# Last mixture of experts: wider token rows, routing straight from the logits, another order of loads, a shared expert in two parts, and sums on three engines

## The chip, the core and the metric

The kernel runs on one core of a Trainium2 chip. The engines are called by short names: PE (TensorE, matrix products), PEld (its weight loads), DVE (VectorE), ACT (ScalarE), POOL (GpSimd), SP (SyncE, which here only issues transfers). The metric is the device time of one execution in microseconds (us); smaller is better. Times given inside an execution are microseconds from the start of its profiled span.

## The reference

Four layers of attention and feed-forward work over x[1024, 256], each followed by a residual sum and a layer norm. The change concerns the last feed-forward, a mixture of 64 experts:

```
logits = h @ router_w.T                       # h: [1024, 256] -> [1024, 64]
probs  = softmax(logits)
top_vals, top_idx = top_k(probs, 8)
top_vals = top_vals / sum(top_vals)
comb   = zeros(1024, 64) with top_vals at top_idx
for each expert e:                            # 2 x 64 hidden columns
    g, u = split(h @ gate_up[e].T)
    out += (silu(g) * u) @ down[e].T * comb[:, e]
shared = sigmoid(h @ shared_gate_w.T) * (silu(h @ Sg.T) * (h @ Su.T)) @ Sd.T
x = layernorm(x + out + shared)
```

## The kernel before, in words

The stages run one after another (`STAGES`). Inside a block under `in_order(transfers=True)` every engine, SP's queue included, executes in the order in which the program is written, so a place in the text is a place in each queue.

**Clearing.** `clear_rows` (L1366 to L1376), called at the start of the feed-forward of the third layer, makes a table in device memory of 64 experts x 1024 rows of `ROW` numbers (L46, here 256 + 3 x 8 = 280, so 1,120 bytes) and fills it with zeros by 64 transfers on POOL's queue.

**Routing, `close` (L1983 to L2085).** It is a generator: every `yield` ends a step, and `close_on` (L2089) makes one step wherever the attention code or its drain calls it, so the routing of a tile of 128 tokens is spread over the last attention's work. Tiles 0 to 3 go two at a time (n = 2), 4 to 7 singly; a generator is made by `add_up` (L2244) once a tile's attention output is summed, and the generators run one after another. The steps for a tile: root of the variance (`power`, L231: a DVE operation and a power on POOL), norm, three steps apart the transposes (L2009), the copy of the transpose (L2013), the router's logits (L181), a full softmax (L2022 to L2029), the eight largest by `max` and `match_replace` (L2033 to L2035, which gives the 0/1 mask `taken`), gates normalised over the eight (L2037 to L2040, `comb`), then two products on PE that count for every token how many earlier tokens chose each expert (L2043, L2047), and the row places (L2054 to L2071). Last, for each tile, a one-hot comparison of 8 x 64 gathers the eight gates in the order of the places (L2076, L2080, L2084). A row thus holds 256 numbers of the token, 8 expert numbers, 8 result addresses, 8 gates. Each tile then goes out by eight indirect scatters on POOL (L151, `table<-w`), one row per token and chosen expert; `close_on` sends one a call, or two once the attention is drained.

**Experts, `ffn3` (L2408).** SP first loads five of eight pieces of the weights (`weights_for`, L2425: two transfers of gate/up and one of down, 512 KB each, for four pairs of experts). `shared_expert` (L2300) is computed whole and added to `k.x`, then `more_blocks` (L2332) works out which experts have more than 128 rows (98 and up) and need extra blocks. `run` (L2598) goes through 16 groups of four experts ("own") and six extra groups ("more") among them. A group's rows are loaded two groups ahead (`load`, L2443; groups 1, 3 and 5 first issue another piece of weights). Each group has two units; a unit is turned on PE (`turn`, L2522, copy on DVE L2524), multiplied with gate and up (`hidden`, L2533, with silu on ACT L2540 and a product on DVE L2541), turned again if it is an extra one (`turn_hidden`), multiplied with the down weights (`down`, L2576), scaled by its gate on ACT (L2582) and scattered by POOL to its result rows (L151, `results<-y,sel`): 64 such scatters for own units, 12 for extra ones. `find` (L2490) picks for each row its address and its gate by comparing the row's eight expert numbers with the expert at hand. After `run`, an `If` (L2629), which is not taken with these inputs, would do further extra blocks; its branch costs each engine some time.

**Last sums, `add_results` (L2633).** Eight loads of 1 MB each bring a tile's eight results per token (the last in four parts); tiles 2, 4 and 6 are summed by three halving additions on DVE (L2643) and one more (L2644), the others by nine products with the identity on PE (L2648). DVE takes the statistics (L2669, L2670), `power` the root, DVE the final product (L2656), and ACT's queue issues the output's write (L2657).

Of the kernel before, what the change touches and what calls it, by code (L numbers as in the profile page):

```python
# [33 lines left out]
P = 128  # L34
# [11 lines left out]
ROW = D + 3 * K3  # L46
# [1894 lines left out]
def attn3(k, a):  # L1941
# [41 lines left out]
    def close(t, n):  # L1983
# [3 lines left out]
        rstd = k.power(stats[t // 4][:, at : at + n, 1], n, LN_EPS, tag="root")  # L1987
        yield
# [5 lines left out]
        rows, probs, comb, order = part(0, ROW), part(560, 64), part(688, 64), part(912, 8)  # L1994
        taken = work[:, 816 : 816 + 32 * (n + 1)].bitcast(BF16)
        taken = taken.rearrange("p (i e) -> p i e", e=E3)
        place = part(928, 8).bitcast(I32)
# [4 lines left out]
        nc.vector.memset(taken[:, n, :], 0.0)  # L2002
        yield
        yield
        yield
# [7 lines left out]
        nc.vector.tensor_copy(k.xT[:, :, PAD + t * P : PAD + (t + n) * P], ps)  # L2013
        yield
# [7 lines left out]
        nc.vector.tensor_reduce(low, logits, axis=AX.X, op=ALU.max, negate=True)  # L2022
        nc.vector.tensor_tensor(probs, logits, low.unsqueeze(2).to_broadcast(shape), ALU.add)
        nc.scalar.activation(probs, probs, AF.Exp)
        nc.scalar.activation(gate, ps[:, :, 64], AF.Exp, scale=-1.0)
        yield
        nc.vector.tensor_reduce(total, probs, axis=AX.X, op=ALU.add)
        nc.vector.reciprocal(inv, total)
        nc.vector.tensor_tensor(probs, probs, inv.unsqueeze(2).to_broadcast(shape), ALU.mult)  # L2029
        yield  # L2030
        for i in range(n):
            top = k.tile("st", [P, 8])
            nc.vector.max(top, probs[:, i, :])  # L2033
            nc.vector.match_replace(comb[:, i, :], top, probs[:, i, :], -1.0)
        nc.vector.tensor_scalar(taken[:, :n, :], comb, 0.0, None, ALU.is_lt)  # L2035
        yield
        nc.vector.tensor_tensor(probs, probs, taken[:, :n, :], ALU.mult)  # L2037
        nc.vector.tensor_reduce(total, probs, axis=AX.X, op=ALU.add)
        nc.vector.reciprocal(inv, total)
        nc.vector.tensor_tensor(comb, probs, inv.unsqueeze(2).to_broadcast(shape), ALU.mult)  # L2040
        yield
# [10 lines left out]
        yield  # L2052

# [4 lines left out]
        nc.vector.tensor_tensor(base, ps[:, n, :], base, ALU.add)  # L2058
        for i in range(n):
            nc.vector.max(order[:, i, :], probs[:, i, :])  # L2060
        yield
# [4 lines left out]
        for i in range(n):  # L2066
            nc.vector.tensor_scalar(
                rows[:, i, D + K3 : D + 2 * K3], dest, float((t + i) * P * K3), None, ALU.add
            )
# [3 lines left out]
        shape = [P, K3, E3]  # L2073
        for i in range(n):
            eq = k.tile("t2", [P, K3, E3])
            nc.vector.tensor_tensor(  # L2076
                eq, probs[:, i, :].unsqueeze(1).to_broadcast(shape),
                order[:, i, :].unsqueeze(2).to_broadcast(shape), ALU.is_equal,
            )
            nc.vector.tensor_tensor(  # L2080
                eq, eq, comb[:, i, :].unsqueeze(1).to_broadcast(shape), ALU.mult
            )
            yield
            nc.vector.tensor_reduce(rows[:, i, D + 2 * K3 :], eq, axis=AX.X, op=ALU.add)  # L2084
            sending.extend((place[:, i, m : m + 1], rows[:, i, :]) for m in range(K3))  # L2085
# [158 lines left out]
    def add_up(g, b, oT):  # L2244
        project_heads(k, b, oT, ws[g][1])
        if g == 3:
            if b % 4 == 0:
                stats[b // 4] = k.tile("st", [P, 4, 2], tag="stats", bufs=2)
            k.add_stats(b, stats[b // 4])
            if b > 3:  # L2250
                k.closing.append(close(b, 1))
            elif b % 2:
                k.closing.append(close(b - 1, 2))
        yield 4 * D * COLUMN
# [6 lines left out]
    with k.in_order(transfers=True):  # L2261
# [30 lines left out]
        for _ in pipe.drain():  # L2292
            close_on()
        k.drained = True
# [5 lines left out]
def shared_expert(k, gate_up, down):  # L2300


    nc = k.nc
    g, u = k.bank(), k.bank()
    for j, ps in enumerate((g, u)):
        for c in range(NC):
            for half in range(2):
                nc.tensor.matmul(
                    ps[64 * half : 64 * half + 64, :],
                    lhsT=gate_up[:, c, 64 * j : 64 * j + 64],  # L2310
                    rhs=k.xcols(c, half * HALF, HALF), start=c == 0, stop=c == NC - 1,
                )
    h = k.tile("shared", [P, HALF])
    nc.scalar.activation(h, g, AF.Silu)
    nc.vector.tensor_tensor(h, h, u, ALU.mult)
    for t in range(4):
        ys = k.wide()
        for half in range(2):
            rows = slice(64 * half, 64 * half + 64)
            nc.tensor.matmul(  # L2320
                ys[:, half * HALF : half * HALF + D], lhsT=h[rows, t * P : (t + 1) * P],
                rhs=down[rows, :], start=True, stop=True,
            )
        for half in range(2):
            at = 4 * half + t
            nc.vector.scalar_tensor_tensor(
                k.x[:, at, :], ys[:, half * HALF : half * HALF + D], k.gate[:, at : at + 1],
                k.x[:, at, :], ALU.mult, ALU.add,
            )


def more_blocks(k, ids, column):  # L2332
# [26 lines left out]
    columns = small([P, 2])  # L2359
# [6 lines left out]
    expert, start, held, row = (small([P, 2]) for _ in range(4))  # L2366
# [41 lines left out]
def ffn3(k, a):  # L2408
# [27 lines left out]
    for lo in range(0, 20, 4):  # L2436
# [6 lines left out]
    def load(group):  # L2443
        kind, g = group
        xr = rows[group] = k.tile("xr", [P, 4, ROW])
        if kind == "own":
            if g in (1, 3, 5):
                weights_for(20 + 2 * (g - 1))
            nc.sync.dma_start(
                out=xr, in_=regions[4 * g : 4 * g + 4, :P, :].rearrange("e p w -> p e w")  # L2450
            )
# [38 lines left out]
    def find(group):  # L2490
# [3 lines left out]
        at = slice(n * g, n * g + n)  # L2494
        mine = ids[:, at] if kind == "own" else keys[:, at]
        waste = (spare if kind == "own" else spare[:, E3:])[:, at]
        eq, both = k.tile("sel", [P, n, K3]), k.tile("sel", [P, n, 2, K3])
        pair, off, index = (k.tile("sel", m) for m in ([P, n, 2], [P, n], [P, n]))
# [5 lines left out]
        nc.vector.tensor_tensor(  # L2504
            both, xr[:, :, D + K3 :].rearrange("p h (w k) -> p h w k", k=K3),
            eq.unsqueeze(2).to_broadcast([P, n, 2, K3]), ALU.mult,
        )
        nc.vector.tensor_reduce(pair, both, axis=AX.X, op=ALU.add)
        nc.vector.scalar_tensor_tensor(
            off, pair[:, :, 0], 0.0, waste, ALU.is_equal, ALU.mult  # L2510
        )
        nc.vector.scalar_tensor_tensor(index, pair[:, :, 0], -1.0, off, ALU.add, ALU.add)
        found[group] = index, pair
# [54 lines left out]
    def down(unit):  # L2568
        (kind, g), i = unit
        hT, ys, yt = hs.pop(unit), k.wide(), k.tile("y", [P, 2, D])  # L2570
        index, pair = found[kind, g]
        halves = [slice(64 * h, 64 * h + 64) for h in range(2)]
        ys = ys.rearrange("p (r n) -> p r n", r=2)
        if kind == "own":
# [5 lines left out]
            for h in range(2):  # L2580
                at = 2 * i + h
                nc.scalar.activation(  # L2582
                    yt[:, h, :], ys[:, h, :D], AF.Copy, scale=pair[:, at, 1:2]
# [9 lines left out]
        nc.scalar.activation(yt[:, 0, :], ys[:, 0, :D], AF.Copy, scale=pair[:, i, 1:2])  # L2593
# [4 lines left out]
    def run(groups):  # L2598
# [5 lines left out]
        turn(units[0])  # L2604
        for at in range(len(units) + 2):
# [6 lines left out]
            if at < len(units):  # L2612
# [3 lines left out]
            if 0 < at <= len(units):  # L2616
# [170 lines left out]
```

## Time and profile before

| what | us |
|---|---|
| median of the three runs shown (2069.09 to 2073.79) | 2070.15 |
| the profiled execution, whole | 2065.07 |
| its span, first to last instruction | 2063.4 |
| PE busy / DVE busy / ACT busy / POOL busy in the span | 1830.1 / 1314.5 / 884.0 / 695.4 |
| mean granted PE clock | 0.950 |

The page's groups give for every line its engine, operation, output and input by the program's names, how often, busy time, mean time of one in ns, and the idle time of that engine just before. Those of the part that is changed:

```profile
L151 POOL DMA_INDIRECT results<-y,sel x76 | 73.9, 973 | 44.0 <-ACT y L2582 25.5
L151 POOL DMA_INDIRECT table<-w x64 | 64.8, 1012 | 49.1 <-DVE root L235 19.4
L1374 POOL DMA_DIRECT2D table<-zero x64 | 34.1, 534 | 132.3 <-DMA table<-zero 132.3
```

A timeline row has the start, the duration, engine, line, operation, output and input, the count merged into the row, and in brackets how long the engine was idle before and what ended that. A row of the windows has the stretch, its length, the busy time and count of PE, PEld, DVE, ACT and POOL, the granted clock, the share of the DMA engines in use, and the rate in GB/s.

### The profile page before, as it was taken

The numbers are of one execution on the slowest core, as the hardware profiler recorded it, in microseconds if no ns is written. First come the engines' busy times: TensorE is split into PE (matmuls) and PEld (weight loads), VectorE is DVE, ScalarE is ACT, GpSimd is POOL, SyncE is SP. The second block draws the span as 40 slices with busy tenths as digits, with TensorE's granted clock in tenths as the row PEclk, the third lists the DMA queues.
The fourth block names the chain that finished last, engine by engine and source line by source line (L and its number), as shares of the span: only waits on it lengthen the run. The fifth ranks groups of instructions, "written<-read, shape, count | busy, mean of one in ns | idle before, by whom it ended". The sixth has DMA issues, their size and how long they took to land. (4 is left out here: it accounts for less than half of the span.)

```text
span 2063.4 us, 26548 instructions
## 1 busy us (share of the span) xinstructions
PE 1830.1 (89%) x8329; PEld 1143.1 (55%) x8329; DVE 1314.5 (64%) x2873; ACT 884.0 (43%) x2410; POOL 695.4 (34%) x934
## 2 busy tenths in 40 slices
PE   8988759699999989989889989999999998885995
PEld 4655535456666666576444344444666655554654
DVE  5788846667876766545467444453667665865573
ACT  3666614445343343445344622227535454331460
POOL 5343222333333332233021131104333325554472
PEclk9999969899999999998999999999999999997897
DMA  6322254344454553401050089970344423446855
GB/s 184 81 69 75 66 164 133 95 110 124 111 146 107 157 148 93 99 10 62 21 175 2 2 348 419 426 307 25 88 115 110 100 54 98 109 106 240 288 181 216
DMA packets 173651, 281.88 MB, mean 137 GB/s; under 512 B 36000, under 2 KB 133664, under 8 KB 164416
## 3 DMA queue, kind: packets, MB, share of 16 engines
q1 hardware_dynamic: 146832, 161.45, 28.4%
q0 software_dynamic: 25520, 117.60, 15.2%
q8 instruction: 70, 1.15, 0.2%
q10 hardware_dynamic: 1152, 1.05, 0.1%
q14 instruction: 77, 0.63, 0.1%
HBM read 87.75 MB, written 109.71 MB: 96 GB/s over the span
## 5 line engine op out<-in xcount | busy, mean ns | idle before, releaser
L174 PE MATMUL bank<-xT,w 128*128 128x512 f32 (+1 forms) x960 | 390.2, 546 | 3.0 <-DVE xT L200 2.8
L389 DVE STREAM_TRANSPOSE turned<-p 128x128 f32<-128x128 f32 (+7 forms) x232 | 283.7, 1223 | 107.0 <-POOL p L285 59.7
L285 POOL TENSOR_SCALAR p<-p,st 128x128 f32<-128x128 f32 (+7 forms) x256 | 190.4, 744 | 462.1 <-DVE st L284 460.6
L292 PE MATMUL wide<-k,q 128*128 128x512 f32 (+3 forms) x768 | 300.9, 502 | 15.4 <-ACT p L277 14.4
L426 PE MATMUL bank<-pt,v 128*128 128x256 f32 x1216 | 287.4, 379 | 13.5 <-DMA pt<-turned 11.1
L426 PEld LDWEIGHTS bank<-pt,v 128*128 128x128 f32 x1216 | 230.9, 195 | 68.6 <-issue 26.8
L174 PEld LDWEIGHTS bank<-xT,w 128*128 128x128 f32 x960 | 183.7, 196 | 147.4 <-issue 129.7
L269 DVE TENSOR_REDUCE st<-wide 128x1 f32<-128x128 f32 (+7 forms) x256 | 193.4, 756 | 42.2 <-PE wide L297 35.5
L292 PEld LDWEIGHTS wide<-k,q 128*128 128x128 f32 x768 | 141.6, 194 | 134.5 <-issue 95.0
L277 ACT ACTIVATE p<-wide,st 128x128 f32<-128x128 f32 (+7 forms) x128 | 94.8, 741 | 239.0 <-DVE st L269 213.4
L277 ACT ACTIVATE p<-wide,st,factor 128x256 f32<-128x256 f32 (+7 forms) x128 | 106.3, 831 | 101.6 <-POOL st L274 96.3
L264 DVE TENSOR_TENSOR wide<-wide,causal 128x128 f32<-128x128 f32 x192 | 56.0, 292 | 104.2 <-PE wide L292 103.3
L807 ACT ACTIVATE e<-wide,st 128x128 f32<-128x128 f32 x256 | 89.8, 377 | 74.6 <-DVE st L815 65.2
L181 PE MATMUL bank<-w,xT 128*128 128x512 f32 (+2 forms) x288 | 116.2, 539 | 3.4 <-DVE xT L2013 2.0
L1682 ACT ACTIVATE pt<-wide 128x1024 f32<-128x1024 f32 (+3 forms) x96 | 75.6, 810 | 69.8 <-PE wide L1676 67.9
L151 POOL DMA_INDIRECT results<-y,sel x76 | 73.9, 973 | 44.0 <-ACT y L2582 25.5
L1685 POOL TENSOR_SCALAR_AFFINE_SELECT pt<-pt 128x256 f32<-128x256 f32 x64 | 25.9, 406 | 183.2 <-ACT pt L1682 182.8
L151 POOL DMA_INDIRECT table<-w x64 | 64.8, 1012 | 49.1 <-DVE root L235 19.4
L1374 POOL DMA_DIRECT2D table<-zero x64 | 34.1, 534 | 132.3 <-DMA table<-zero 132.3
L181 PEld LDWEIGHTS bank<-w,xT 128*128 128x128 f32 x288 | 52.1, 195 | 47.2 <-issue 37.5
L1634 DVE TENSOR_REDUCE st<-wide 128x2 f32<-128x1024 f32 x64 | 64.3, 1020 | 18.1 <-PE wide L1623 8.9
L873 PE MATMUL bank<-w,ot 128*128 128x256 f32 x256 | 64.6, 398 | 7.8 <-ACT ot L867 5.3
(401 smaller groups left out, 3237.5 us busy)
## 6 DMA issues: line engine op xcount, KB each, us to landing
table<-zero POOLq DMA_DIRECT2D x64, 1120.0 KB, 21.9
pt<-turned SPq DMA_DIRECT2D x60, 240.0 KB
pt<-turned SPq DMA_DIRECT2D x60, 176.0 KB
pt<-turned SPq DMA_DIRECT2D x156, 64.0 KB
xr<-table SPq DMA_DIRECT2D x16, 560.0 KB
gu<-in_L_ffn_gate_up_dram SPq DMA_DIRECT2D x16, 512.0 KB
pt<-turned SPq DMA_DIRECT2D x28, 256.0 KB
r<-results SPq DMA_DIRECT2D x7, 1024.0 KB
```

Of the source, the lines that this page charges most:

```text
L151: self.nc.gpsimd.indirect_dma_start(out=views.pop(), out_offset=bass.IndirectOffsetOnAxis(ap=index, axis=0), in_=source, in_offset=None,)
L174: self.nc.tensor.matmul(out, lhsT=weight(c), rhs=self.xcols(c, lo, n), start=c == 0, stop=c == NC - 1)
L181: self.nc.tensor.matmul(out, lhsT=self.xcols(c, lo, n), rhs=weight(c), start=c == 0, stop=c == NC - 1)
L269: nc.vector.tensor_reduce(top, scores[:, :n], axis=AX.X, op=ALU.max, negate=True)
L277: nc.scalar.activation(probs[:, :n], scores[:, :n], AF.Exp, bias=top, scale=1.0 if scale is None else scale, accum_out=total,)
L285: self.nc.gpsimd.tensor_scalar(probs[:, :n], probs[:, :n], total, 1.0, ALU.mult, ALU.mult)
L292: self.nc.tensor.matmul(s[:, lo : lo + m], lhsT=query, rhs=key(lo, m), start=True, stop=not masked or lo + m < n, skip_group_check=masked,)
L389: k.nc.vector.transpose(squares.rearrange("p b (k q) -> p b k q", q=32), probs[:, :n].rearrange("p (k i b) -> p b k i", b=4, i=32),)
L426: self.k.nc.tensor.matmul(out.rearrange("p (a q) -> p a q", q=32) if first else out.rearrange("p (s a q) -> p s a q", s=2, q=32), lhsT=val ...
L807: nc.scalar.activation(e[:, r, f, b, :], sc[:, r, f, b, :], AF.Exp, bias=top[:, at : at + 1], accum_out=total[:, at : at + 1],)
L873: nc.tensor.matmul(y, lhsT=oT[:, i % 2 * 2 + i // 2].rearrange("p b n -> p (b n)"), rhs=wo[:, i, :], start=i == 0, stop=i == 3,)
L1682: nc.scalar.activation(two[:, :, lo:], sc[:, :, lo:], AF.Exp)
```

## The change

Rows carry all 64 gates instead of eight picked ones, so `ROW` is 256 + 16 + 64 = 336 numbers (1,344 bytes), the one-hot gathering goes, and `comb` is written straight into the row. The eight largest are found among the logits; the exponent is taken with the largest subtracted, and only the masked exponents are summed. The steps of `close` are fewer and in another order, the last tile's root is issued at once in `add_up`, and the drain makes two steps per call. In `ffn3` six pieces of weights precede the rows, the first group's rows come in two transfers, and groups 1 and 3 issue their piece of weights after their rows. `find` reads the gate from the row's column, or for extra groups selects it among 64. Own units go to `down` one round sooner. The shared expert's gate half is computed before `run` and the rest after it. The last sums go to PE (tiles 1, 4, 7), POOL (2, 5) and DVE (0, 3, 6); the root is ACT's square root, and ACT makes the final product.

```diff
-ROW = D + 3 * K3
+ROW = D + 2 * K3 + E3
...
-    def close(t, n):
+    def close(t, n, rstd=None):
-        rstd = k.power(stats[t // 4][:, at : at + n, 1], n, LN_EPS, tag="root")
-        yield
+        if rstd is None:
+            rstd = k.power(stats[t // 4][:, at : at + n, 1], n, LN_EPS, tag="root")
+            yield
...
+        comb = rows[:, :, D + 2 * K3 :]
...
-        yield
-        yield
+        if n > 1:
+            yield
+            yield
...
+        nc.vector.memset(taken[:, n, :], 0.0)
+        for i in range(n):
+            nc.vector.tensor_scalar(
+                rows[:, i, D + K3 : D + 2 * K3], dest, float((t + i) * P * K3), None, ALU.add
+            )
...
-        nc.vector.tensor_reduce(low, logits, axis=AX.X, op=ALU.max, negate=True)
-        nc.vector.tensor_tensor(probs, logits, low.unsqueeze(2).to_broadcast(shape), ALU.add)
-        nc.scalar.activation(probs, probs, AF.Exp)
...
+        for i in range(n):
+            nc.vector.max(order[:, i, :], logits[:, i, :])
+            nc.vector.match_replace(probs[:, i, :], order[:, i, :], logits[:, i, :], NEG)
+        nc.vector.tensor_tensor(taken[:, :n, :], probs, logits, ALU.not_equal)
+        nc.vector.tensor_scalar(low, order[:, :, 0], -1.0, None, ALU.mult)
         yield
         for i in range(n):
+            nc.scalar.activation(probs[:, i, :], logits[:, i, :], AF.Exp, bias=low[:, i : i + 1])
+        nc.scalar.activation(gate, ps[:, :, 64], AF.Exp, scale=-1.0)
...
-        for i in range(n):
-            eq = k.tile("t2", [P, K3, E3])
...
-            yield
-            nc.vector.tensor_reduce(rows[:, i, D + 2 * K3 :], eq, axis=AX.X, op=ALU.add)
...
+            if b == NT - 1:
+                rstd = k.power(stats[b // 4][:, b % 4 :, 1], 1, LN_EPS, tag="root")
+                k.closing.append(close(b, 1, rstd))
...
         for _ in pipe.drain():
             close_on()
+            close_on()
...
-    for lo in range(0, 20, 4):
+    for lo in range(0, 24, 4):
         weights_for(lo)
...
         if kind == "own":
-            if g in (1, 3, 5):
-                weights_for(20 + 2 * (g - 1))
-            nc.sync.dma_start(
-                out=xr, in_=regions[4 * g : 4 * g + 4, :P, :].rearrange("e p w -> p e w")
-            )
+            step = 4 if g else 2
+            for lo in range(0, 4, step):
+                at = 4 * g + lo
+                nc.sync.dma_start(
+                    out=xr[:, lo : lo + step, :],
+                    in_=regions[at : at + step, :P, :].rearrange("e p w -> p e w"),
+                )
+            if g in (1, 3):
+                weights_for(22 + 2 * g)
             return
...
+        combs = xr[:, :, D + 2 * K3 :]
+        if kind == "own":
+            scales = [combs[:, i, n * g + i : n * g + i + 1] for i in range(n)]
+        else:
...
+            nc.vector.tensor_tensor(
+                picked, ids.unsqueeze(1).to_broadcast(shape),
+                mine.unsqueeze(2).to_broadcast(shape), ALU.is_equal,
+            )
+            nc.vector.tensor_tensor(picked, picked, combs, ALU.mult)
+            nc.vector.tensor_reduce(scale, picked, axis=AX.X, op=ALU.add)
...
         turn(units[0])
+        hidden(units[0])
+        find(units[0][0])
...
-            if 0 < at <= len(units):
-                turn_hidden(units[at - 1])
-            if at > 1:
-                down(units[at - 2])
+            for unit in units[at - 1 : at] if at else ():
+                if unit[0][0] == "own":
+                    down(unit)
+                else:
+                    turn_hidden(unit)
+            for unit in units[at - 2 : at - 1] if at > 1 else ():
+                if unit[0][0] != "own":
+                    down(unit)
...
-        shared_expert(k, shared, shared_down)
+        shared = Shared(k, shared, shared_down)
         where, keys, sides, longest = more_blocks(k, ids, column)
+        shared.gate()
...
         run([group for _, group in sorted(own + more)])
+        shared.up()
+        shared.add()
...
+    def sums(t, e):
         r, y = rs[t], k.x[:, t, :]
...
+    def measure(t):
+        six, two = k.tile("st", [P, 6]), k.tile("st", [P, 2])
+        nc.vector.bn_stats(six, ys[t])
+        nc.vector.bn_aggr(two, six)
+        root = k.tile("st", [P, 1])
+        nc.scalar.activation(root, two[:, 1:], AF.Sqrt, bias=k.eps[LN_EPS])
+        stats[t], roots[t] = two, root
+
+    def finish(t):
+        root, shift, z = roots[t], k.tile("st", [P, 1]), k.tile("z", [P, D])
+        nc.vector.reciprocal(root, root)
+        nc.vector.scalar_tensor_tensor(shift, stats[t][:, :1], -1.0, root, ALU.mult, ALU.mult)
+        nc.scalar.activation(z, ys[t], AF.Identity, bias=shift, scale=root)
+        nc.sync.dma_start(out=k.out[t * P : (t + 1) * P, :], in_=z)
...
+        for lo, n in ((0, 4), (4, 2), (6, 2)):
+            load(NT - 1, lo, n)
+        for t in (1, 4, 7):
+            sums_on_pe(t)
+        for t in (2, 5):
+            sums(t, nc.gpsimd)
+        sums(0, nc.vector)
+        measure(0)
+        measure(1)
+        finish(0)
+        sums(3, nc.vector)
+        finish(1)
+        measure(2)
+        measure(3)
+        finish(2)
+        finish(3)
+        measure(4)
+        sums(6, nc.vector)
+        finish(4)
+        measure(6)
+        measure(5)
+        finish(6)
+        measure(7)
+        finish(5)
+        finish(7)
```

`Shared.gate` projects the shared expert's gate half and applies silu, `Shared.up` projects the other half and multiplies, `Shared.add` multiplies with the down weights and adds to `k.x`; they hold the operations of `shared_expert`.

## The prediction

> **What bounds the kernel now.** I read the slices first (the change touches only the last 170 us of 2063.4, and the clearing of the table near 1200 to 1380), then the chain of waits there, POOL's timeline, and the windows. The chain shows what starts the experts:
> ```profile
> 1906.36 2.44 DMA table<-w
> 1908.86 0.38 SPq L2449
> 1910.91 8.23 DMA xr<-table
> ```
> The last row scatter starts at 1906.36, lands 2.44 us later, only then is the first row read issued; the second read waits 8.23 us behind 1.5 MB of weights. How the last tile comes so late, and what follows it, is in the timeline:
> ```profile
> 1883.38 0.14 DVE L235 TENSOR_SCALAR root<-stats 128x1 f32<-128x1 f32 x1
> 1896.06 0.69 DVE L2084 TENSOR_REDUCE w<-t 128x8 f32<-128x512 f32 x1
> 1897.51 0.96 POOL L151 DMA_INDIRECT table<-w  x1 [3.31 <-issue]
> ...
> 1926.49 0.95 POOL L151 DMA_INDIRECT results<-y,sel  x1 [19.17 <-ACT y L2582]
> ...
> 2024.31 0.96 POOL L151 DMA_INDIRECT results<-y,sel  x1 [0.30 <-issue]
> ...
> 2027.92 17.33 SPq L2665 DMA_DIRECT2D r<-results  x11
> ...
> 2059.95 0.54 DVE L2656 TENSOR_SCALAR z<-bank,st,st 128x256 f32<-128x256 f32 x1 [0.44 <-POOL st L236]
> ```
> Tile 7's root waits for tile 6's gate gathering; its own ends at 1896.75. The results' scatters run from 1926.49 to 2025.27: 98.8 us for 76, where 76 x 1.266 (pitch: 0.96 busy, 0.30 idle) is 96.2. So POOL sets the experts' end, and its first scatter sets POOL. After that the reads take 2.46 us a tile, and DVE works until 2060.49, 11 us after the last read.
>
> **The end of attention: costed at 0.** The gate gathering goes (0.67 + 0.69 + 0.64 = 2.0 us of DVE a tile), and so does the full softmax (five operations, some 1.0 us). Rows are sent six steps sooner. Why this may pay:
> ```profile
> 1849.66 1.99 DVE L389 STREAM_TRANSPOSE turned<-p 128x1024 f32<-128x1024 f32 x1 [3.87 <-POOL p L285]
> ...
> 1853.99 0.69 PE L2009 MATMUL bank<-ident,x 128*128 128x128 f32 x2 [3.64 <-DVE st L284]
> ```
> Three scatters (1844.89 to 1848.47) stood on POOL before the product that DVE waited for, and PE stood 3.64 us. Against it: single tiles lose two empty steps before their transposes, so PE, in written order, reaches them sooner and waits on the norm sooner. A stall removed is worth 3.64, plus the slow clock after it (scores 3.62 against 1.88, sixteen value products 5.06 against 3.67), in all 6.8. Bounds: 6.8 gained, or 6.8 lost on each of tiles 4, 5 and 6. I take 0, as both ends rest on the same stall.
>
> **Tile 7's rows.** Its root follows its statistics (1881.26): +0.21 to the DVE operation, +0.25 to POOL's power, +0.60 to the norm, all as for tile 6 from 1852.46: 1882.32, before 1886.69. From norm to first use of the logits 2.96 as before: 1885.28. Then maximum, replacement and mask 0.82 (1891.16 to 1891.98), the negated maximum 0.19, exponent on ACT 0.4, four operations to the gates 1.07, the ranks 1.1: 1888.9. Then 0.76 to the first scatter, as from 1896.75 to 1897.51: 1889.6, which is 7.9 sooner. Tile 6's eight scatters (10.1 us) fit into POOL's idle 19.45 us before 1883.74. Tile 7's eighth starts at 1898.5; those from 1883 to 1900 took 5.5 to 6.2 us to land beside weights, so 1904.3.
>
> **The reads still wait, for the weights ahead of them.** Six pieces stand ahead instead of five: 6 x 1.573 MB, 0.26 for the shared expert, 8 x 0.172 for tile 7's scatters (rows of 1,344 bytes for 1,120): 11.08 MB.
> ```profile
> 1880.00:1890.00 10.00, 2.08 (x8) 1.22 (x6) 4.30 (x12) 0.41 (x1) 5.13 (x6) 0.69 1.00 359
> 1890.00:1900.00 10.00, 5.81 (x18) 1.82 (x18) 6.35 (x25) 2.19 (x4) 5.21 (x6) 0.63 1.04 403
> ```
> The last two columns are DMA share and GB/s: full. They carry 7.62 MB by 1900; the other 3.46 at 403 GB/s end at 1908.6. Half a group (0.344 MB) takes 0.85, and 0.15 to PE: the first turn at 1909.6, before 1913.18. The other rows follow at once, so the 2.24 us that PE stood before 1919.27 go too. Bounds: 1905.5, if rows overtake weights, and 1913, if nothing is won. What moves on SP's queue: the sixth piece's three issues (1.6 us as at 1909.29 to 1910.86) fall into its idle 1893.5 to 1908.8, one more read issue costs 0.4 behind the full DMA queue, nothing on the path; the last pieces' issues now stand behind reads.
>
> **To the first result.** PE at its slow clock: turn 0.97, wait for the copy 0.85, products 1.98, two turns 1.94, products 1.9, then 1.43 from the start of the down product (1925.06) to the scatter (1926.49): 9.1. First scatter 1918.7, 7.8 sooner; the same 98.8 us bring the last to 2017.5. PE as a check: it took 105.45 us (1913.18 to 2018.63), less 2.24: 2012.8, plus about 3 for the last copies and scatters, 2015.8. POOL stays ahead of it as the bound, by little. Bounds for POOL's gaps: none (2014.9), or PE no longer ahead and 7 us of gaps (2021.9, the wait for a first result being 7.8 less than it was).
>
> **Costed at nothing.** Clearing: 20% more bytes. The fills' pitch is 2.93 us (161.1 over 55), so 55 x 0.59 = 32.2 us more.
> ```profile
> 1359.69 0.53 POOL L1374 DMA_DIRECT2D table<-zero  x1 [2.29 <-DMA table<-zero]
> 1396.09 1.03 POOL L236 TENSOR_TENSOR st<-st,minus_half 128x4 f32<-128x4 f32 x1 [35.87 <-DVE st L235]
> ```
> The queue behind them is free until 1396.09; the last fill would be issued by 1392.4 and land by 1418, before the next transfer on SP's queue (1427.29). The cover is 3.7 us; every further us is lost. Extra groups pick their gate from 64: three operations of 0.29 (L2362, L2367) six times, 5.2 us of DVE, which is busy 7.13 of 8 us at its fullest there; POOL's backlog covers it. Last weights behind the rows: units 24 and up come late. Up projection and sum after the run: 2.7 (half of 5.47) + 0.8 + 3.34 = 6.8 us from 2012.8 to 2019.6, and DVE's branch 3.1 (2017.6 to 2020.7): 2022.7, against a first result tile at 2024.9. If that cover goes, up to 4 us of DVE's wait for PE's first sum covers the rest. ACT's table loads once more (1.28, as at 1897.53), in that same wait. The eight output writes go from ACT's queue to SP's, idle after the reads.
>
> **The last sums.** Reads start 2.65 us after the last scatter ends: R = 2020.2. Tiles land at R + 4.7, then each 2.46 (R + 21.9 for the last). DVE adds three tiles at 2.86 each and measures eight (0.65); power on POOL is replaced by a root on ACT and two small DVE operations (0.35); the 0.47 of the product moves to ACT. New waits: ACT's product waits for DVE's shift, and a later tile's root queues behind it on ACT, for which DVE's next reciprocal waits: 0.5 at most each, and only in the last two tiles without other DVE work between. PE's tile 1, cold, ends at R + 13.2 as tile 0 took 6.1, so DVE's third starts at 14.3. POOL's adds: 1.27 for 512 elements (L1895), so 5.1 a tile, R + 9.6 to 14.7 and 17.0 to 22.1. Freely, DVE's order then ends in z at R + 27.3. But two engines add at once, and this trace shows what that does:
> ```profile
> 122.31 3.27 DVE L823 SCALAR_TENSOR_TENSOR diff<-e,st 128x128 f32<-128x128 f32 x4
> 122.32 2.60 POOL L627 TENSOR_TENSOR k<-t,t 64x512 f32<-64x512 f32 x2
> ...
> 132.05 1.14 DVE L823 SCALAR_TENSOR_TENSOR diff<-e,st 128x128 f32<-128x128 f32 x4
> ```
> The four DVE operations take 1.14 alone and 3.27 beside POOL. At R + 17.1 the small products of tile 1's and later shifts stand behind POOL's 2.54, 1.27 and twice 0.64, and tile 6's add slips with them: about 2.4, z at R + 29.7. With 2.9 from the last z to the end (as 2060.49 to 2063.4): R + 32.6, where before took 35.5. I take the locked value; the bounds are 30.2, and 36 if every DVE addition waits.
>
> The Trainium skill (SBUF — State Buffer, "Who interferes with whom") says that a DVE instruction with two SBUF inputs contends with a GpSimd one that reads SBUF, and that whoever issues first keeps the port for a whole instruction. It speaks against giving POOL a share of the sums: by it each such DVE addition can lose up to one POOL instruction. The row above agrees; by the rule the sum is the locked one, without it 2.4 us less.
>
> **Sum.** 2020.2 + 32.6 = 2052.8 against the span of 2063.4: 10.6 us less, of which 7.8 lie before R and 2.9 after it. That execution took 2065.07, the runs shown have a median of 2070.15. Rounding the saving to 11: 2059.
>
> **Rivals.** More: the stall at 1850 goes, with its clock, 6.8, and the lock costs nothing, 2.4: 2050. For it: POOL's three scatters would be sent before. Against: the shorter way to the transposes. Hidden: PE, not POOL, ends the experts, since it no longer runs 13 us ahead of the first scatter; 7 of 7.8 us come back as gaps on POOL and only the tail's 2.9 stay: 2070.15 - 3.7 = 2066.5. For it: from 1990 PE is busy 8.00, 7.87 and 8.00 of 8 us. Against: POOL is at its pitch for the first 48 scatters. Slower: the transposes, two steps sooner, stop PE on the norms of tiles 4, 5 and 6 in turn, 6.8 us each with the clock: 2059 + 20.4 = 2079. It decides from 3.7 us a tile on; PE already stood 2.14, 2.67 and 3.64 there. Against: it was the late scatters that made the longest of them. Does not do what it says: the fills outgrow their cover, 40% slower instead of 20%: 55 x 1.17 = 64 us later less 35.9 of cover, 28: 2087.
>
> **How the numbers follow.** Forecast 0.60 (its own range 2052 to 2065), more 0.18, hidden 0.10, slower by stalls 0.09, by fills 0.03. Within 0.2% (4.1 us, about what a measurement of this kernel can tell) is 2066.0 to 2074.3: that is the hidden case. Faster 0.78, same 0.10, slower 0.12. The range 2048 to 2068 takes in the forecast, the hidden case and most of "more".
>
> **What would show it.** First results scatter near 1918.7 after the same attention, first turn near 1909.6, 76 scatters in 97 to 101 us, reads-to-end 32 to 33 us, POOL's power near 1396 unmoved. Wrong it is if PE's waits on the transposes grow past 3.7 us a tile, if the fills end after 1396, or if POOL shows more than 7 us of gaps between results.

## The result, and the profile after

Timed beside each other on one chip, the changed kernel takes 2077.32 us (median of 15, 2070.99 to 2086.41) and the kernel before 2067.13 us (median of 15, 2060.18 to 2074.73): ratio 1.005, 95% interval 1.0033 to 1.0068. The change costs some 10 us where 11 us less were forecast. The profiled execution of the changed kernel took 2070.99 us, the least of its 15; its span is 2069.3 us.

Three places split both spans into four stretches: POOL's first power of attn3 (1396.09 before, 1391.84 after), the first transposed transfer on SP's queue (1427.29 and 1441.52), the addition of tile 7's attention output (line L255, 1880.34 and 1894.04), and the first read of results (2027.92 and 2035.96).

| stretch | before | after | difference |
|---|---|---|---|
| power to first transposed transfer | 31.20 | 49.68 | +18.5 |
| from there to tile 7's addition | 453.05 | 452.52 | -0.5 |
| tile 7's addition to first result read | 147.58 | 141.92 | -5.7 |
| first result read to the end | 35.5 | 33.3 | -2.1 |

The sum, +10.2, is as large as the difference of the medians (up to the power this execution happened to be 4.3 us ahead, so the spans differ by 5.9). So the last two stretches, at which the change aims, did gain 7.8 us in these two executions. The loss stands 450 us ahead of them, at the start of the last attention. This is the timeline of the changed kernel there:

```profile
1385.44 0.53 POOL L1374 DMA_DIRECT2D table<-zero  x1 [2.73 <-DMA table<-zero]
1387.15 8.85 PE L181 MATMUL bank<-w,xT 128*128 128x512 f32 x20 [1.47 <-DVE xT L200]
1389.23 0.59 ACT L2095 COPY q<-bank 128x512 f32<-128x512 f32 x1 [1.71 <-PE bank L181]
1391.84 1.03 POOL L236 TENSOR_TENSOR st<-st,minus_half 128x4 f32<-128x4 f32 x1 [5.87 <-DVE st L235]
1411.17 0.59 ACT L2095 COPY q<-bank 128x512 f32<-128x512 f32 x1 [19.62 <-DMA table<-zero]
1411.81 7.82 PE L181 MATMUL bank<-w,xT 128*128 128x512 f32 x12 [15.81 <-ACT q L2095]
1413.78 1.01 POOL L236 TENSOR_TENSOR st<-st,minus_half 128x4 f32<-128x4 f32 x1 [19.79 <-DVE st L235]
```

The last of the 64 fills is issued at 1385.44, in time, and POOL's power at 1391.84 is not late: the queue was free, as forecast. But ACT's second copy (tile 1's raw rows, out of PSUM into a tile `q`) waits 19.62 us, and what ends its wait is a transfer from `zero` to `table`. PE waits 15.81 us behind it for a free bank of PSUM, the memory that its products go to. The windows of the same execution show the whole core standing:

```profile
1390.00:1400.00 10.00, 6.00 (x14) 2.30 (x13) 0.17 (x1) 1.45 (x8) 2.07 (x2) 0.98 1.01 429
1400.00:1410.00 10.00, 0.00 (x0) 0.00 (x0) 0.00 (x0) 0.00 (x0) 0.00 (x0) 0.50 0.78 330
1410.00:1420.00 10.00, 8.19 (x17) 3.80 (x18) 0.58 (x3) 8.13 (x31) 5.78 (x6) 0.67 0.01 2
```

From 1400 to 1410 no engine does anything; only DMA works, at 330 GB/s. The allocation of the built program says why a copy of attention rows should wait for zeros: the tile `zero` lies at bytes 103,424 to 114,176 of each partition, and the tile `q` of tile 1's raw rows at 103,424 to 105,472. The fills read the zeros until the last packet at 1410.57, and only then may ACT overwrite them. In the kernel before the two tiles start at the same address too, but there the last packet of the fills is through at 1381.24, and the first two copies run without a wait for them:

```profile
1393.48 0.58 ACT L2110 COPY q<-bank 128x512 f32<-128x512 f32 x1 [1.71 <-PE bank L181]
1395.78 0.58 ACT L2110 COPY q<-bank 128x512 f32<-128x512 f32 x1
```

The rows that answer to the others of the prediction, from the timelines of the changed kernel (SP, PE, POOL, DVE; two answers put in order of time):

```profile
1895.42 0.57 POOL L236 TENSOR_TENSOR root<-root,minus_half 128x1 f32<-128x1 f32 x1 [6.28 <-DVE root L235]
1902.43 1.04 POOL L151 DMA_INDIRECT table<-w  x1 [6.44 <-issue]
1917.32 1.77 SPq L2451 DMA_DIRECT2D xr<-table  x3
1924.41 1.12 PE L2535 MATMUL bank<-ident,xr 128*128 128x128 f32 x4 [12.15 <-DMA xr<-table]
1933.80 0.96 POOL L151 DMA_INDIRECT results<-y,sel  x1 [21.39 <-ACT y L2595]
2029.69 3.34 DVE L2327 SCALAR_TENSOR_TENSOR x<-wide,w,x 128x256 f32<-128x256 f32 x8 [0.89 <-PE wide L2320]
2030.72 0.96 POOL L151 DMA_INDIRECT results<-y,sel  x1 [0.30 <-issue]
2035.96 1.12 SPq L2665 DMA_DIRECT2D r<-results  x2
```

Counted from tile 7's addition, tile 7's first table scatter comes 8.39 us later (before 17.17), the first turn 30.37 (32.84), the first scatter of results 39.76 (46.15), the first result read 141.92 (147.58).

### The profile page after: what moved, and what is told of

Read it like the earlier page. It is cut to its first block, busy times and chain, and to the rows that moved or that the text cites. A ratio compares the mean times of both kernels' runs of the same rounds, so it can differ in the third digit from the quotient of the medians.

```text
span 2069.3 us, 26495 instructions
## 1 busy us (share of the span) xinstructions
PE 1816.2 (88%) x8293; PEld 1132.2 (55%) x8293; DVE 1298.5 (63%) x2843; ACT 892.6 (43%) x2429; POOL 703.0 (34%) x934
## 5 line engine op out<-in xcount | busy, mean ns | idle before, releaser
L174 PEld LDWEIGHTS bank<-xT,w 128*128 128x128 f32 x960 | 183.2, 195 | 147.6 <-issue 128.2
L181 PE MATMUL bank<-w,xT 128*128 128x512 f32 (+2 forms) x288 | 117.8, 543 | 17.8 <-ACT q L2095 15.8
```

Of the source, the lines that this page charges most:

```text
L174: self.nc.tensor.matmul(out, lhsT=weight(c), rhs=self.xcols(c, lo, n), start=c == 0, stop=c == NC - 1)
L181: self.nc.tensor.matmul(out, lhsT=self.xcols(c, lo, n), rhs=weight(c), start=c == 0, stop=c == NC - 1)
```

## Experiments

Theory "held memory": the fills hold the memory of the zeros, and the copy that reuses it waits. Rivals: the DMA traffic itself stops the stage, POOL's queue does, or other parts of the change do. The kernels ran in four groups, each on another chip, and on three of these chips the kernel before takes 34 to 39 us more than its 2067 us; what can be said of that stands in the last section. So each row of this table is compared with the kernel before on its own chip ("before"), and the stretches come from the profiled run.

| run | before | time | ratio (95%) | power to transfer | addition to read | read to end |
|---|---|---|---|---|---|---|
| e1_zero_elsewhere | 2106.24 | 2102.23 | 0.9997 (0.9979 to 1.0016) | 31.2 | 180.7 | 33.0 |
| e2_wide_clear_before | 2106.24 | 2123.14 | 1.0094 (1.0073 to 1.0114) | 49.0 | 176.6 | 34.6 |
| after_same_chip | 2101.26 | 2126.14 | 1.0121 (1.0098 to 1.0145) | 49.2 | 187.4 | 34.4 |
| e1_same_chip | 2101.26 | 2105.34 | 1.0021 (1.0002 to 1.0039) | 31.2 | 181.8 | 34.0 |
| e3_five_pieces | 2101.26 | 2103.01 | 1.0005 (0.9987 to 1.0022) | 31.2 | 184.0 | 33.3 |
| e4_shared_first | 2101.26 | 2104.31 | 1.0009 (0.9990 to 1.0028) | 31.2 | 188.8 | 34.1 |
| e5_sums_without_pool | 2067.64 | 2057.11 | 0.9950 (0.9929 to 0.9972) | 31.2 | 144.6 | 32.3 |
| e6_all_mended | 2067.64 | 2050.18 | 0.9925 (0.9903 to 0.9947) | 31.2 | 136.6 | 31.3 |
| before_same_chip | 2067.64 | 2068.90 (one) | | 31.2 | 145.7 | 34.8 |
| after_for_trace | 2067.64 | 2082.39 (one) | | 47.4 | 142.5 | 33.2 |
| e1_third_chip | 2105.34 | 2102.74 | 1.0002 (0.9982 to 1.0021) | 31.2 | 180.8 | 34.7 |
| after_third_chip | 2105.34 | 2126.61 | 1.0097 (1.0073 to 1.0121) | 49.1 | 182.2 | 33.9 |

**The zeros elsewhere.** A tile of 34,816 bytes is put ahead of the zeros, of which one column is written:

```diff
+    gap = k.tile("gap", [P, 17 * HALF])
+    k.nc.gpsimd.memset(gap[:, :1], 0.0)
     zero = k.tile("zero", [P, REGION // P * ROW])
...
-    ffn2: dict(p4=3, t2=8, zero=1),
+    ffn2: dict(p4=3, t2=8, gap=1, zero=1),
```

> The changed kernel with one difference: 34,816 bytes a partition are left free ahead of the tile of zeros, so that it lies over memory that attn3 first writes near 1434 us, and no longer under the raw rows of tile 1. Nothing is computed otherwise. Theory 'held memory' (the copy of tile 1's raw rows waits until the last fill has read the zeros): the 19.62 us wait of the L2095 copy on the fills goes, from POOL's first power of attn3 to the first transposed transfer on SP's queue it takes 31 to 32 us as in the kernel before, not 49.7; fills as before in time; the time falls by 17 to 19 us from 2077.3, to 2058 to 2061, a ratio of 0.996 to 0.997 to the kernel before. Rival 'traffic' (the fills' DMA traffic itself stops the stage, whatever memory the zeros lie in): the stretch stays at 48 to 50 us and the time at 2077, ratio 1.005. Rival 'POOL's queue' (the power stands behind the fills): the power moves to after 1396, the time stays at 2075 to 2079.

The stretch is 31.20 us, exactly that of the kernel before, and no copy waits for the fills. The ratio, 0.9997, misses the expectation (0.996 to 0.997): from tile 7's addition to the first read this execution took 180.7 us, the changed kernel in its first measurement 141.9. Without the changed kernel on the same chip that could not be read, so both were run together, twice.

> The changed kernel with the zeros elsewhere, once more, beside the changed kernel itself. Theory 'held memory': 17 to 19 us less than the changed kernel beside it, all of it between the power and the first transposed transfer (31 to 32 us against 49 to 50); on a chip where the experts' scatters take 97 to 99 us the ratio to the kernel before is 0.996. Rival 'given back': the stage is shorter and what follows is longer by as much (on the other chip the scatters took 135 us): less than 8 us between the two.

> The changed kernel as it is, timed on the same chip as the three beside it, since the run with the zeros elsewhere fell on a chip where the kernel before took 2106, not 2067, and both kernels lost 28 to 37 us among the experts. Theory 'held memory': power to first transposed transfer 49 to 50 us, ratio to the kernel before 1.004 to 1.006 (on a chip with slow experts up to 1.009). Rival 'chip': the loss belongs to the chip of the first measurement: ratio at or under 1.000 here.

> The changed kernel with the zeros elsewhere, alone, for its share of the gain of 'all mended' (0.9925). If the parts add up (8.0 us for the other three mends): 2058 to 2060 where the kernel before takes 2067, ratio 0.995 to 0.997; on a chip with late releases (before over 2095) 0.998 to 1.003. Rival 'the three others did it': ratio at or over 1.000 where the kernel before takes 2067.

> The changed kernel beside it on the same chip. Theory 'held memory': 17 to 21 us more than with the zeros elsewhere; ratio to the kernel before 1.004 to 1.007 where that takes 2067, 1.010 to 1.014 on a chip with late releases. Rival: under 8 us between the two.

The differences of the medians are 2126.14 - 2105.34 = 20.8 us and 2126.61 - 2102.74 = 23.9 us, above the 17 to 19 and the 17 to 21 expected; the rivals had under 8. The two pairs of profiled spans differ by 21.9 and 22.6 us: 18.0 and 17.9 of it are the stretch, 5.6 and 1.5 lie between tile 7's addition and the first read, and the rest (-1.7 and +3.2) elsewhere. The ratios of the changed kernel, 1.0121 and 1.0097, lie above the 1.009 allowed for in the first case and just under the 1.010 of the second. The windows of e1_same_chip, whose power is at 1400.87, around the place at which the changed kernel stood:

```profile
1390.00:1400.00 10.00, 7.58 (x29) 3.88 (x28) 6.44 (x20) 3.81 (x10) 1.60 (x3) 1.00 1.01 423
1400.00:1410.00 10.00, 10.00 (x24) 4.32 (x23) 0.89 (x4) 8.34 (x34) 8.21 (x8) 1.00 1.01 429
1410.00:1420.00 10.00, 9.72 (x33) 4.01 (x31) 1.29 (x2) 5.29 (x9) 0.00 (x0) 1.00 1.01 428
```

Behind the power PE is busy 10.00 and 9.72 of 10 us while the DMA engines show a busy share of 1.01 with the same fills, which run on until 1424.66. So neither the traffic nor the bytes stop the stage: the place of the zeros alone does. That rules out the rival "traffic"; the rival "POOL's queue" falls too, as the power follows its copy by 2.6 us here, in the kernel before and in the changed one. The new place (bytes 138,240 to 148,992) has a cover of its own: the first transposed transfer writes over it, at 1432.07, 7.4 us behind the last packet.

**The fills alone, in the kernel before.** The zeros get 2,688 numbers, the fills clear a table of 20% more memory; rows and reads stay.

```diff
-    k.table = k.tile("dram", [E3 * REGION, ROW], tag="table")
+    wide = REGION // P * 336
+    table = k.tile("dram", [E3 * P, wide], tag="table")
+    flat = table.rearrange("p w -> (p w)")
+    k.table = flat[: E3 * REGION * ROW].rearrange("(r w) -> r w", w=ROW)
...
-    zero = k.tile("zero", [P, REGION // P * ROW])
+    zero = k.tile("zero", [P, wide])
...
-        rows = k.table[e * REGION : (e + 1) * REGION, :]
-        k.nc.gpsimd.dma_start(
-            out=rows.rearrange("(p r) w -> p (r w)", p=P), in_=zero
-        )
+        k.nc.gpsimd.dma_start(out=table[e * P : (e + 1) * P, :], in_=zero)
```

> The kernel before with one difference: the zeros are 2,688 numbers a partition as in the changed kernel, not 2,240, and the 64 fills clear a table of 20% more memory; rows, scatters and everything read stay as before. Theory 'held memory': fills end near 1411 us, the copy of tile 1's raw rows waits 16 to 19 us for them, power to first transposed transfer takes 47 to 50 us, not 31.2, and the kernel is 15 to 19 us slower than before: 2082 to 2086, ratio 1.0075 to 1.009. Rival 'hidden' (as the prediction had it, the cover holds, and the loss of the changed kernel comes from its other parts): 2066 to 2068, ratio 0.999 to 1.001. Rival 'other parts of the attention' (shorter way to the transposes, earlier sends): also 0.999 to 1.001.

The ratio is 1.0094, just above the 1.0075 to 1.009 expected, and the stretch 49.0 us. The waits of this run from 1385 to 1440 (engine, tile and line waiting, what ended it, sum in us, count, longest):

```profile
ACT q L2110 <- DMA table<-zero: 18.4, 1, 18.4
PEld bank L181 <- ACT q L2110: 15.4, 1, 15.4
PE bank L181 <- ACT q L2110: 14.6, 1, 14.6
```

The same copy (here L2110) waits for the same fills, though nothing else of the change is in this kernel. So 20% more bytes, by themselves, make the loss: 17.8 us of stretch, of the 18.5 in the changed kernel.

**Five pieces of weights ahead of the rows** (on the kernel with the zeros elsewhere):

```diff
-    for lo in range(0, 24, 4):
+    for lo in range(0, 20, 4):
...
-            if g in (1, 3):
-                weights_for(22 + 2 * g)
+            if g in (1, 3, 5):
+                weights_for(18 + 2 * g)
```

> The changed kernel with the zeros elsewhere, and five weight pieces ahead of the row reads, not six (the sixth, seventh and eighth follow the rows of groups 1, 3 and 5). Theory 'the queue ahead' (rows wait for whatever weights were issued before): 1.573 MB less at 403 GB/s is 3.9 us: from tile 7's add to the first turn 26 to 27 us, not 30.3; as POOL's scatters follow the first result, 3.5 to 4 us less than the kernel with the zeros elsewhere. Rival 'late weights': the units that use the sixth piece wait as long as was won: 0 to 1 us less. Rival 'rows late themselves' (the reads wait on the scatters' landing): first turn within 1 us of 30.3.

From tile 7's addition to the first turn it takes 26.55 us against 30.38 in e1_same_chip: 3.8 sooner, as "the queue ahead" has it. The time is 2.3 us less, not 3.5 to 4, and the two intervals overlap; from the addition to the first read the profiled run even took 2.2 us more (184.0 for 181.8). On that chip the time decides nothing.

**The shared expert first** (also on it): `shared.up()` and `shared.add()` are called right behind `shared.gate()`.

> The changed kernel with the zeros elsewhere, and the shared expert's up projection, product and additions to x ahead of the routed experts, where PE and DVE stand idle for some 12 us, not after them. Theory 'branch behind the additions' (the first result read waits for DVE's branch, which stands behind the additions): from the last scatter's end to the first result read 2.6 to 2.7 us, not 4.3, so 1.5 to 1.7 us less than the kernel with the zeros elsewhere. Rival 'start pushed back': the 5 us of PE and 3 us of DVE come on top of the first turn: 1 to 4 us more. Rival 'nothing': the read waits for the landing of the last scatters: 0.

From the last scatter's end (2065.88 + 0.96) to the first read at 2069.74 it takes 2.9 us, in e1_same_chip 4.5; the first turn moves by 0.4 only (30.8). So the branch did stand behind DVE's additions, and ahead of the first turn their new place costs next to nothing. The time, 1.0 us less, is again inside the intervals, and the profiled run took 7.0 us more from the addition to the first read (188.8 for 181.8): what the new place costs among the experts is not shown on that chip.

**No sums on POOL** (also on it): DVE sums tiles 0, 2, 4 and 6, PE the others, and DVE's steps are ordered s0 m0 s2 f0 m2 m1 f2 s4 f1 m4 m3 f4 s6 f3 m5 m6 f5 f6 m7 f7 (s sum, m `measure`, f `finish`).

> The changed kernel with the zeros elsewhere, and the last sums of tiles 0, 2, 4, 6 on DVE and 1, 3, 5, 7 on PE, none on POOL; DVE's order is written anew for it. Theory 'lock' (DVE's operations stand behind POOL's additions): no 128x1 operation of DVE in the tail over 0.5 us (2.11 in the changed kernel), each DVE sum of a tile near 2.9 us, first result read to the end 30 to 31 us, not 33.0 to 34.4; 2 to 3.5 us less than the kernel with the zeros elsewhere. Rival 'POOL's share is needed' (DVE and PE have too much without it): the tail stays at 33 us or more, 0 to 2 us more in all.

In the changed kernel's tail, timeline rows of DVE and POOL:

```profile
2047.68 5.42 POOL L2670 TENSOR_TENSOR r<-r 128x1024 f32<-128x1024 f32 x3 [16.00 <-DMA r<-results]
2051.30 3.21 DVE L2670 TENSOR_TENSOR r<-r 128x1024 f32<-128x1024 f32 x3
2054.70 4.62 POOL L2670 TENSOR_TENSOR r<-r 128x1024 f32<-128x1024 f32 x3 [0.47 <-DMA r<-results]
2055.08 2.11 DVE L2693 SCALAR_TENSOR_TENSOR st<-st,st 128x1 f32<-128x1 f32 x1
```

and in the tail of e5_sums_without_pool:

```profile
2038.38 2.41 DVE L2672 TENSOR_TENSOR r<-r 128x1024 f32<-128x1024 f32 x3 [1.78 <-DMA r<-results]
2041.36 0.16 DVE L2695 SCALAR_TENSOR_TENSOR st<-st,st 128x1 f32<-128x1 f32 x1
2050.77 3.72 PE L2679 MATMUL bank<-r,ident 128*128 128x256 f32 x16 [0.92 <-DMA r<-results]
2054.53 0.43 DVE L2686 BATCH_NORM_STATS2 st<-bank 128x6 f32<-128x256 f32 x1 [1.42 <-PE bank L2679]
```

The lock is real: an operation on one number a partition takes 2.11 us beside POOL's additions and 0.16 without them, three DVE additions 3.21 and 2.41. But the tail became 32.3 us, not 30 to 31. DVE now waits for PE and PE for the reads: PE's last products end 27.4 us after the first read, so reads and PE's sum of tile 7 set the end. Against the 33.2 to 33.3 of the changed kernel 1.0 to 1.1 is won; DVE and PE do POOL's share in its place, so this is the net of both, and what the lock costs by itself is not shown.

**All four together.**

> All four mends together: zeros elsewhere, five weight pieces ahead of the rows, shared expert whole ahead of the routed ones, no sums on POOL. If the parts add up: 18.5 + 3.9 + 1.6 + 2.5 = 26.5 us less than the changed kernel. Where the experts' scatters take 98 us (the kernel before at 2067) that is 2051, a ratio of 0.992; on a chip like the two of the last runs, where the changed kernel is at 1.0121, 0.9995. Rival 'late releases eat it' (PE's completions reach ACT and DVE late whatever stands ahead): no better than the kernel with the zeros elsewhere, ratio 1.000 to 1.002 there.

2050.18 us where 2051 was expected, ratio 0.9925: this version beats both kernels. The zeros alone were not timed on such a chip; from e5_sums_without_pool (2057.11, 1.0 less in the tail) they come to about 2058, an estimate. The four together were not run on a chip of the other kind, so the second expectation stays open, and so does the rival to it. The first turn comes 26.8 us after tile 7's addition, the first scatter of results 34.9, the first read 136.6.

**The two kernels on that chip, for their traces.**

> The kernel before as it is, for its trace on this chip. Theory 'the experts lose by the chip': if it takes over 2095 us here, all of the excess over 2067 lies between the first and the last scatter of results (125 us or more, not 98.8), and the stage from power to first transposed transfer takes 31.2 us as on the first chip. Rival 'clock': the excess is spread over all stages (2% of each).

> The changed kernel as it is, for its trace beside that of the kernel before on one chip. Theory 'held memory': power to first transposed transfer 49 to 50 us. From tile 7's add to the end the changed kernel is 7.8 us shorter if the chip is like the first; if the scatters take over 120 us in both, the difference there has either sign, and the theory says nothing on it.

The chip was of the first kind: the kernel before at 2068.90, its stretches within 3.2 us of those of its first profile (31.2, 456.2, 145.7 and 34.8), 95.9 us from the first to the last start of a result scatter. The condition of its expectation (over 2095 us) was not met. The changed kernel has 47.4 us in the first stretch where 49 to 50 was expected (its copy waits 18.14 us), and is 180.56 - 175.72 = 4.8 us shorter from tile 7's addition to the end, where 7.8 was expected: one execution of each, and the kernel before was 2.5 us quicker there than in its first profile (183.0).

## Why the prediction was wrong

**The step that failed** is the clearing under "Costed at nothing". Its sizes were good: 32.2 us more were forecast for the fills, from first issue to last packet they grew by 33.8 (187.5 to 221.3); the last issue was put at 1392.4 and came at 1385.44, in an execution that was 4.3 us ahead. What was wrong is the cover: "The queue behind them is free until 1396.09", and behind it SP's queue until 1427.29. Both queues were indeed free. But a third user stood behind the fills, the next owner of the memory that they read. Measured by that, the cover in the kernel before is from the last packet at 1381.24 to the copy of tile 1's rows at 1395.78: 14.5 us, not the 35.9 that POOL's queue had. The fills grew by 33.8; 19.3 is left, and the wait is 19.62. Of it 18.5 reached the stretch.

**The rival with the right sign**, fills that outgrow their cover, was put at 28 us and a chance of 0.03 by the wrong place, POOL's queue, and by fills 40% slower where 18% was measured (221.3 for 187.5). The sentence "every further us is lost" was right only once the cover was counted to the right owner.

**Attention's end, taken at 0**: -0.5 us, and 3.2 us lie between two profiles of the kernel before (453.05 and 456.21). The number held, though not for the reason given. PE's waits ahead of the transposes of tiles 4, 5 and 6 were 2.14, 2.67 and 3.64 us and are 4.99, 2.99 and 3.14. So both ends came at once, each small: tile 4's transposes now wait longer for their norm (`x` of L228), past the 3.7 us that the prediction had named, and 0.5 of the 3.64 that was to go went. For the two tiles ahead of them the wait fell from 2.32 to 0.25. The changes of these waits add up to +0.6; that they cancel was luck.

```profile
1794.52 0.69 PE L2011 MATMUL bank<-ident,x 128*128 128x128 f32 x2 [4.99 <-DVE x L228]
```

**Tile 7's rows**: 8.8 us sooner (17.17 to 8.39 after the addition), forecast 7.9.

**The queue of weights ahead of the rows**: the mechanism was right, the first turn is 1.1 us later than forecast (30.37 for 29.3). e3_five_pieces shows that one piece is worth 3.8 us, worked out from the rate as 3.9.

**The experts**: 97.9 us for the scatters where 98.8 was taken; POOL's pitch stayed the bound on the first chip, so "hidden" did not happen.

**Shared expert behind the run, costed at nothing**: 1.6 us lost. The prediction set DVE's additions against the landing of the first result tile. But the issue of that read stands behind the branch, and SP's waits in the changed kernel name DVE there:

```profile
SPq L2665 <- DVEq L2650: 1.7, 1, 1.7
```

The additions end at 2033.03, the last scatter at 2031.68; the read came 4.3 us after it, not 2.65, and e4_shared_first brings it back to 2.9.

**The tail**: 33.3 for 32.6. The taken value held, but its reason only in part, so the agreement is partly luck. The Trainium skill (SBUF — State Buffer, "Who interferes with whom") has the DVE instruction wait while a GpSimd instruction holds the shared port; the rows agree (2.11 us for an operation of 0.16). That this makes 2.4 us of tail was too much: without POOL 1.0 to 1.1 is won, as the reads come in as late as before.

Together: forecast -10.6 from tile 7's addition on, measured -7.8 (-4.8 in the second pair of profiles); forecast 0 at the start of attention, measured +18.5. No run tested the change of `find` or the extra groups' gate by itself.

## What to carry over

A transfer that "nobody waits for" still holds the memory it reads until its last packet. Whoever makes it longer has to look for three things behind it: what follows on its queue, who reads what it writes, and which later tile is laid over its source; the last is in the allocation and not in the text of the kernel. Moving the source to memory that is needed later cost no time that shows and gave back the whole stall here (31.20 us again).

## What the runs showed of the hardware

**Late releases on some chips.** The kernel before took 2067 us in the first measurement and in one of the four groups, and 2101 to 2106 in the other three, on other chips. The last attention is not clearly slower there (451.5 to 457.0 us from the first transposed transfer to tile 7's addition, against 452.5 to 456.2 on the first kind). Most of the excess lies among the experts: by the spans after_same_chip is 53.2 us longer than the first profile of the changed kernel, 45.5 of it from tile 7's addition to the first read (187.4 for 141.9) and 8.1 ahead of the power. Of the kernel before no profile was taken on such a chip; its variant e2_wide_clear_before is 29.0 us longer in that stretch than its first profile (176.6 for 147.6). ACT's rows in the first profile of the changed kernel:

```profile
1936.90 0.28 ACT L2553 ACTIVATE s<-bank 128x128 f32<-128x128 f32 x1 [0.77 <-PE bank L2546]
1939.15 0.28 ACT L2553 ACTIVATE s<-bank 128x128 f32<-128x128 f32 x1 [0.77 <-PE bank L2546]
1941.39 0.28 ACT L2553 ACTIVATE s<-bank 128x128 f32<-128x128 f32 x1 [0.77 <-PE bank L2546]
```

and in after_same_chip, the same program:

```profile
1946.52 0.28 ACT L2553 ACTIVATE s<-bank 128x128 f32<-128x128 f32 x1 [2.83 <-PE bank L2546]
1950.97 0.28 ACT L2553 ACTIVATE s<-bank 128x128 f32<-128x128 f32 x1 [2.21 <-PE bank L2535]
1956.10 0.28 ACT L2553 ACTIVATE s<-bank 128x128 f32<-128x128 f32 x1 [3.56 <-remote]
```

The wait for PE's product is 0.77 each time in the first rows and 2.2 to 3.6 in the second ("remote": the profile names nothing that ended the wait). The product for which ACT starts at 1946.52 ends by the record at 1943.82; its signal is recorded at 1946.49, together with those of three later groups of PE. In the 80 us from the first scatter of results on, the signal of a PE group's end comes over 0.3 us behind the recorded end in 3 of 118 cases in the first profile and in 38 of 78 in after_same_chip, often several at once. The Trainium skill (Perfetto Trace Analysis, "Tensor Engine Instruction (MATMUL, LD_WEIGHTS)") says that the profile's end of a matrix product is estimated, and that the signal follows later, outside the record; which part of that is late here these runs do not show. From the first to the last start of a result scatter it takes 97.8 us in the kernel before and 96.9 in the changed one in their first profiles, 126.7 in e2_wide_clear_before, and 135 to 145 in the runs with the changed order of work on such chips. So part of the change's gain seems to be taken back there: the changed kernel's ratio is 1.0097 to 1.0121, on the first chip 1.005. Why these chips, and why among the experts, is open.
